# Shorter chains for identity, lengths and mask in the first group, roots in nine operations, and a tie between query scaling and late weights

## The chip, the cores and the metric

The kernel runs on one core of a Trainium2 chip. The metric is device time in microseconds of one execution, from first to last instruction with what lies around them. A core has a matrix engine (TensorE, PE; its weight loads are listed as PEld), a vector engine (VectorE, DVE), an activation engine (ScalarE, ACT), a general engine (GpSimd, POOL), and SyncE (SP), which here issues nearly all DMAs. Each engine works through its own queue in order. TensorE writes to PSUM, which has eight banks[...].

## The reference, cut to what matters

A stack of four graph layers with residual and layer norm, on x of 3327 x 256 and an adjacency matrix of 3327 x 3327. The change touches the first layer, a masked attention with cosine scores, and the inverse square root that all layers use:

```python
def _cos_normalize(x):
    n = jnp.linalg.norm(x, axis=-1, keepdims=True)
    return x / jnp.maximum(n, COS_EPS)
Qn = _cos_normalize(features @ Wq.T)
Kn = _cos_normalize(features @ Wk.T)
raw_att = Kn @ Qn.T
att = jnp.where(adj > 0, raw_att, NEG) * TEMP
att = jax.nn.softmax(att, axis=1)
prop_fea = att @ features
adj_mask = (jnp.sum(adj, axis=1) > 0).astype(features.dtype)[:, None]
prop_fea = adj_mask * prop_fea + (1.0 - adj_mask) * features
# ... then 0.5 * prop_fea + 0.5 * features, and
x = _layernorm(x + _L0_gnn_ref(x, adj, L0_gnn_Wq, L0_gnn_Wk), axis=-1)
```

The later layers (a graph attention, a dot-product attention, three stacked graph attentions) follow with the same mask.

## The kernel before, in words

The 3327 rows are padded to NT = 26 tiles of 128. A block b is a group of four tiles (512 columns; the last has two), so there are NB = 7 blocks. For every layer and block a loop runs over the 26 tiles j. One step (layer, b, j) makes the weights e of tile j against block b, and multiplies them with the value tile V[j] into PSUM accumulators po. In layer 0 `weights0` makes e: a matmul ps of FT[j // 4] (half 0, unscaled) against FT[b] (half 1, normalized), an exponential on ACT whose scale is the inverse length rq of tile j, and a product with the 0/1 mask on DVE. `make` runs three steps ahead of the products (LA = 2, plus one). Blocks 1 to 5 of layer 0 and all of layer 2 use a seven-product scheme: two steps' weights are joined by sums on DVE (`sums`) and used together on the odd step, so on even steps no e is taken from the queue.

Before block 0 can start, the kernel must have: an identity matrix for transposes (a row count, doubled on DVE, four matmuls on TensorE that turn it, and a comparison; eight warm-up matmuls on a tile of ones run ahead of them, L80); FT[0], from `queries0(0)` and `keys0(0)`; the first mask; and the first tiles of x. `queries0` makes the projections pk, sums their squares on ACT, takes inverse lengths (`lengths`, which calls `rsqrt`), scales (L364 on DVE, L366 on ACT), transposes (pkT, L370) and copies to FT[g][:, 1] (L371). `keys0` makes the projection pq (L305), squares it (L312), copies it to FT[g][:, 0] (L313), sums the squares over partitions by matmuls pn (L317), and turns them into rq. Both are generators: each `next` traces the part up to the next `yield`. For g = 0 they are interleaved by hand; for g > 0 parts of them run beside the steps of the block before, and `queries0` takes its inverse lengths on GpSimd, followed by 4 (g = 1) or 7 bare yields until the scaling.

`rsqrt` starts from the integer trick and makes three Newton steps: 11 instructions on DVE, 14 on GpSimd, each waiting for the one before; `lengths` adds a maximum in front.

`take_adj` turns a stage of adjacency (two tiles, 128 x 1024 int32) into a mask of bytes, on DVE for the first eight tiles of block 0 (L408), on ACT (Relu, Sign: L411, L412) otherwise, and adds the stage to a running sum on DVE (L416, L420). `load_adj` loads the next stage; there are three stage buffers.

What sets the order: up to step 3 of the first block the engines PE, ACT, DVE and POOL keep the order in which instructions are written. After that a scheduler orders each engine's instructions, by the written order among those that it takes to be ready by its own model of durations; so an instruction whose inputs it believes to be early can be moved ahead of others on its engine. DMAs queue on SP in order. PSUM: five banks for po, three for everything else (`bank`), given out as they come free.

Of the kernel before, what the change touches and what calls it, by code (L numbers as in the profile page):

```python
# [8 lines left out]
F32 = mybir.dt.float32  # L9
# [4 lines left out]
AF = mybir.ActivationFunctionType  # L14
# [19 lines left out]
def gnn_stack(ctx: ExitStack, tc: tile.TileContext, a: dict, N: int, out: bass.AP):  # L34
# [15 lines left out]
    def bw(b):  # L50
        return min(CH, NP - b * CH)
# [14 lines left out]
    def bank(name):  # L66
        return ps_b.tile([P, CH], F32, tag="pb", name=name)
# [8 lines left out]
    nc.vector.memset(ones, 1.0)  # L76

    turned = bank("turned")
    for _ in range(8):
        nc.tensor.matmul(turned[:, :P], ones, ones, start=True, stop=True)  # L80

    count = const.tile([P, P], F32, name="count")
    nc.vector.memset(count[:, 0:1], 1.0)
    n = 1
    while n < P:
        nc.vector.tensor_scalar(
            count[:, n : 2 * n], count[:, :n], float(n), None, ALU.add
# [43 lines left out]

    def rsqrt(dst, v, n, eng=nc.vector, tag="rs"):

        g = cols.tile([P, n], I32, tag=tag + "_g", name="rs_g")
        eng.tensor_scalar(g, v.bitcast(I32), -0.5, MAGIC, ALU.mult, ALU.add)
        y = g.bitcast(F32)
        vh = cols.tile([P, n], F32, tag=tag + "_v", name="rs_v")
        eng.tensor_scalar(vh, v, -0.5, None, ALU.mult)
        for k in range(3):
            q = cols.tile([P, n], F32, tag=tag + "_q", name="rs_q")  # L140
            eng.tensor_tensor(q, y, y, ALU.mult)
            eng.tensor_tensor(q, q, vh, ALU.mult)
            z = dst if k == 2 else cols.tile([P, n], F32, tag=tag + "_y", name="rs_y")
            if eng is nc.vector:
                eng.scalar_tensor_tensor(z, q, 1.5, y, ALU.add, ALU.mult)
            else:
                eng.tensor_scalar(q, q, 1.5, None, ALU.add)
                eng.tensor_tensor(z, q, y, ALU.mult)
            y = z


    def times(wt, v):
# [114 lines left out]
    def setups():  # L267
        for g in (setup1(), setup2(), setup3a()):
            yield from g
            yield  # L270
# [23 lines left out]
    def lengths(dst, v, n, eng=nc.vector, tag="rs"):  # L294

        eng.tensor_scalar(v, v, COS_EPS * COS_EPS, None, ALU.max)
        rsqrt(dst, v, n, eng, tag)

    def keys0(g):

        wd, n = bw(g), len(tiles_of(g))
        xT = xTs[g]
        pm = bank("pq")
        for h in range(2):
            nc.tensor.matmul(  # L305
                pm[:, :wd], w["qk"][:, h, :H], xT[:, h, :wd], start=(h == 0), stop=(h == 1)
            )
            if g == 1 and h == 0:
                yield
        yield  # L310
        sq = work.tile([P, CH], F32, tag="u", name="qsq", bufs=2)
        nc.scalar.activation(sq[:, :wd], pm[:, :wd], AF.Square)  # L312
        nc.scalar.copy(FT[g][:, 0, :wd], pm[:, :wd])  # L313
        yield
        pn = bank("pn0")
        for k in range(n):
            nc.tensor.matmul(  # L317
                pn[:, k : k + 1], sq[:, k * P : (k + 1) * P], ones[:, :1], start=True, stop=True
            )
        yield  # L320
        v = cols.tile([P, 4], F32, tag="qss", name="qss")
        nc.scalar.copy(v[:, :n], pn[:, :n])
        lengths(rq[:, 4 * g : 4 * g + n], v[:, :n], n)

    def queries0(g):

        wd, n = bw(g), len(tiles_of(g))
        xT = xTs[g]
        ss = cols.tile([P, 4], F32, tag="kss", name="kss")
        kr = work.tile([P, 4, H], F32, tag="kr", name="kr", bufs=1)  # L330
        banks = [bank("pk") for _ in range(2 if g == 0 else 1)]
        for k in range(n):
            pk = banks[k // 2 if g == 0 else 0][:, k * H : (k + 1) * H]
            for h in range(2):
                nc.tensor.matmul(
                    pk,
                    xT[:, h, k * P : (k + 1) * P],
                    w["qk"][:, h, H:],
                    start=(h == 0),
                    stop=(h == 1),  # L340
                )
        if g > 0:
            nc.scalar.copy(kr.rearrange("p k n -> p (k n)")[:, :wd], banks[0][:, :wd])
            yield
        src = [
            banks[k // 2][:, k * H : (k + 1) * H] if g == 0 else kr[:, k, :] for k in range(n)
        ]
        for k in range(n):
            jk = work.tile([P, H], F32, tag="sq0", name="sq", bufs=1)
            nc.scalar.activation(jk, src[k], AF.Square, accum_out=ss[:, k : k + 1])  # L350
        yield
        rk = cols.tile([P, 4], F32, tag="rk", name="rk")
        if g == 0:
            lengths(rk[:, :n], ss[:, :n], n)
        else:
            lengths(rk[:, :n], ss[:, :n], n, nc.gpsimd, "prs")
            for _ in range(4 if g == 1 else 7):
                yield
        yield
        for k in range(n):  # L360
            if g > 0 and k == 2:
                yield
            if g == 0 and k >= 2:
                nc.vector.tensor_scalar(kr[:, k, :], src[k], rk[:, k : k + 1], None, ALU.mult)  # L364
            else:
                nc.scalar.mul(kr[:, k, :], src[k], rk[:, k : k + 1])  # L366
        yield
        pt = bank("pkT")
        for k in range(n):
            nc.tensor.transpose(pt[:, k * P : (k + 1) * P], kr[:, k, :], ident)  # L370
        nc.scalar.copy(FT[g][:, 1, :wd], pt[:, :wd])  # L371
# [7 lines left out]
    def mask(b, j, n=1):  # L379
        wd = bw(b)  # L380
        return masks[b][:, j * wd : (j + n) * wd]
# [21 lines left out]
    def take_adj(b, j):  # L403

        wd = bw(b)
        st = stages.pop((b, j))[:, : 2 * wd]
        if b == 0 and j < 8:
            nc.vector.tensor_scalar(mask(b, j, 2), st, 0, None, ALU.is_gt)  # L408
        else:
            t_ = work.tile([P, 2 * CH], BF16, tag="a", name="pos", bufs=3)  # L410
            nc.scalar.activation(t_[:, : 2 * wd], st, AF.Relu)  # L411
            nc.scalar.activation(mask(b, j, 2), t_[:, : 2 * wd], AF.Sign)  # L412
        if j == 0:
            acc = work.tile([P, CH], I32, tag="u", name="acc", bufs=2)
            adj_sum[b] = acc[:, :wd]
            nc.vector.tensor_tensor(adj_sum[b], st[:, :wd], st[:, wd:], ALU.add)  # L416
        else:
            acc = adj_sum[b]
            for h in range(2):
                nc.vector.tensor_tensor(  # L420
                    acc, acc, st[:, h * wd : (h + 1) * wd], ALU.add
                )
# [30 lines left out]
    def weights0(b, j):  # L453
        wd = bw(b)
        if j % 2 == 0:
            take_adj(b, j)
            load_adj()
        ps = bank("ps")
        nc.tensor.matmul(  # L459
            ps[:, :wd],  # L460
            FT[j // 4][:, 0, (j % 4) * P : (j % 4 + 1) * P],
            FT[b][:, 1, :wd],
            start=True,
            stop=True,
        )
        t_ = work.tile([P, CH], F32, tag="a", name="ex", bufs=3)

        nc.scalar.activation(  # L468
            t_[:, :wd], ps[:, :wd], AF.Exp, scale=rq[:, j : j + 1]
        )  # L470
        return masked(b, j, t_)

    gq = {}

# [730 lines left out]
    load_adj()  # L1205
    masks[0] = new_mask(0)
    k0, q0, q1 = queries0(0), keys0(0), keys0(1)
    for part in (k0, q0, k0, q0, q0, k0, k0, q0, q1):
        next(part, None)
    make(0)  # L1210
    next(q1)
    make(1)
    prep = iter(())
    kprep = iter(())
    setup = setups()
    pre = iter(())

# [10 lines left out]
    for s, (L, b, j) in enumerate(steps):  # L1228
# [29 lines left out]
        if L.key == "0" and b < NB - 1:  # L1258
# [6 lines left out]
            if j >= at + 3:  # L1265
                next(kprep, None)
        es = None if end else made.popleft()
        if end:

            k, h = divmod(2 * j, NT)  # L1270
            for i in (h, h + 1):
                nc.tensor.matmul(  # L1272
                    pos[k],
                    made[i][:, k * P : (k + 1) * P],
                    V[1][i],
                    start=(i == 0),
                    stop=(i == NT - 1),
                )
            if j == 0:
                xm = fetch_last()  # L1280
            if j == NT // 2 - 1:
                ends.append(finish_last(pos[0], xm, 0))
            if ends:
                next(ends[0], None)
        elif not strassen(L, b):
            for k in range(len(pos)):
                nc.tensor.matmul(  # L1287
                    pos[k],
                    es[:, k * P : (k + 1) * P],
                    V[L.i % 2][j],  # L1290
                    start=(j == 0),
                    stop=(j == NT - 1),
                )
        elif j % 2:
            products(pos, b, j // 2, es, V[L.i % 2])
# [115 lines left out]
```

## Time and profile before

| what | value |
|---|---|
| time, median of 3 runs (lowest to highest) | 2379.34 us (2378.32 to 2379.5) |
| the profiled execution's own time | 2376.0 us |
| its span | 2374.2 us |
| mean granted clock of TensorE | 0.998 |
| HBM read, written | 167.53 MB, 28.19 MB |
| first matmul; first L1287 matmul (po) | 1.05 us; 16.38 us |
| POOL memset of 1 column; of 256 columns | 98 ns; 0.31 to 0.34 us |

The time of the profiled execution is some 3 us below the median of the runs, so sums are made against the former. TensorE's busy share is 9 tenths or more in all 40 slices but the last:

```profile
PE   9999999999999999999999999999999999999997
DVE  7889999866666657567567685556656555655665
ACT  4667776765555422222222255555655555655554
POOL 0000001000000000000000000000000000000000
```

Each digit is the busy share of one fortieth of the span (59 us), in tenths. The start shows in the DMA view of the first 60 us: the transfers run at some 370 GB/s from about 3 us to 14 us and with gaps after that. By the semaphores in the trace the projection weights have landed at 4.52 us, the first half of xT's first group at 4.85, its second half at 5.59, the first stage of adjacency at 8.36, the second at 11.13, the third at 12.46.

### The profile page before, as it was taken

How to read it: one execution, taken by the hardware profiler on the slowest of the kernel's cores; microseconds unless marked ns; L12 is line 12 of the kernel's file. 1: busy time of each engine (PE TensorE's matmuls, PEld its weight loads, DVE VectorE, ACT ScalarE, POOL GpSimd, SP SyncE). 2: the span in 40 equal slices, each digit the busy share in tenths (PEclk: the TensorE clock that was granted, in tenths of full speed). 3: DMA queues.
4: the chain of work that ended last, by engine and by line, in shares of the span. 5: the costliest groups of instructions: out<-in, count | busy, mean ns of one | idle time of the engine just before them, and what ended most of it. 6: DMA issues, size and time to landing. Idle time of an engine off the chain costs nothing.

```text
span 2374.2 us, 33168 instructions
## 1 busy us (share of the span) xinstructions
PE 2345.3 (99%) x11965; PEld 1913.6 (81%) x11965; DVE 1608.6 (68%) x4318; ACT 1221.7 (51%) x1959; POOL 42.0 (2%) x168
## 2 busy tenths in 40 slices
PE   9999999999999999999999999999999999999997
PEld 6777877888888777667667798888888888888886
DVE  7889999866666657567567685556656555655665
ACT  4667776765555422222222255555655555655554
POOL 0000001000000000000000000000000000000000
PEclk9999999999999999999999999999999999999999
DMA  8655555422232312212212221210211111132120
GB/s 264 197 180 185 168 196 180 158 84 83 74 83 57 105 56 87 79 53 88 74 49 73 82 85 50 73 52 26 76 47 43 43 59 52 43 98 69 60 66 23
DMA packets 147288, 214.66 MB, mean 90 GB/s; under 512 B 76093, under 2 KB 101172, under 8 KB 142516
## 3 DMA queue, kind: packets, MB, share of 16 engines
q1 hardware_dynamic: 146852, 212.28, 28.9%
q8 instruction: 94, 1.54, 0.3%
q14 instruction: 70, 0.57, 0.1%
q10 hardware_dynamic: 272, 0.26, 0.0%
HBM read 167.53 MB, written 28.19 MB: 82 GB/s over the span
## 4 chain that ended last, share of the span: by engine, by line
PE 89%; DVE 6%; ACT 2%; DMA 2%; issue 1%; POOL 0%; DVEq 0%; ACTq 0%; SPq 0%; POOLq 0%
PE po L1287 49%; PE po L739 17%; PE ps L523 12%; PE ps L459 4%; PE pproj L948 4%; DVE e L448 1%; PE pv L1034 1%; DMA turned<-planes 1%; PE pgq L482 1%; DVE acc L420 1%; PE po L1272 1%; DMA stage<-in_adj_a 1%; DVE ejunk L551 1%; PE pq L305 0%; DVE y L882 0%
## 5 line engine op out<-in xcount | busy, mean ns | idle before, releaser
L1287 PE MATMUL po<-v,e 128*128 128x257 f32 x5616 | 1251.8, 381 | 1.9 <-ACT p L917 1.1
L1287 PEld LDWEIGHTS po<-v,e 128*128 128x128 f32 x5616 | 1062.1, 190 | 169.2 <-issue 9.6
L617 ACT ACTIVATE re<-u,nrh,th 128x512 f32<-128x512 f32 (+1 forms) x728 | 556.4, 780 | 482.7 <-DVE e L628 477.9
L628 DVE SCALAR_TENSOR_TENSOR e<-re,rh,mask 128x512 f32<-128x512 f32 (+1 forms) x702 | 502.3, 719 | 376.7 <-PE po L1287 353.4
L448 DVE SCALAR_TENSOR_TENSOR e<-ex,mask 128x512 f32<-128x512 f32 (+1 forms) x364 | 235.3, 649 | 197.1 <-ACT ex L531 158.2
L523 PE MATMUL ps<-gT,ft 128*128 128x512 f32 (+1 forms) x728 | 307.4, 563 | 0.0
L531 ACT ACTIVATE ex<-ps,off 128x512 f32<-128x512 f32 (+1 forms) x182 | 119.0, 655 | 355.6 <-PE ps L523 329.0
L739 PE MATMUL po<-tsums,ssum 128*128 128x128 f32 (+1 forms) x1794 | 250.9, 275 | 1.7 <-DVE ssum L689 1.4
L739 PEld LDWEIGHTS po<-tsums,ssum 128*128 128x128 f32 x1794 | 224.8, 192 | 3.6 <-DVE ssum L689 3.0
L739 PEld LDWEIGHTS po<-v,e 128*128 128x128 f32 x1196 | 169.4, 191 | 69.2 <-issue 52.9
L523 PEld LDWEIGHTS ps<-gT,ft 128*128 128x128 f32 x728 | 132.1, 190 | 114.5 <-issue 111.7
L739 PE MATMUL po<-v,e 128*128 128x129 f32 x1196 | 182.7, 275 | 1.8 <-DVE e L448 1.8
L468 ACT ACTIVATE ex<-ps,rq 128x512 f32<-128x512 f32 (+1 forms) x182 | 118.0, 653 | 108.2 <-PE ps L459 99.4
L459 PE MATMUL ps<-ft,ft 128*128 128x512 f32 (+1 forms) x312 | 142.7, 562 | 1.1 <-ACT ex L468 1.1
L420 DVE CUSTOM_DVE_ANT_0 acc<-acc,stage 128x1024 uint16<-128x1024 uint16 (+1 forms) x168 | 108.7, 647 | 10.3 <-DMA stage<-in_adj_a 6.4
L739 PE MATMUL po<-v,ssum 128*128 128x128 f32 x598 | 92.3, 275 | 0.0
L739 PE MATMUL po<-tsums,e 128*128 128x128 f32 x598 | 92.2, 275 | 0.0
L412 ACT ACTIVATE mask<-pos 128x1024 uint8<-128x1024 bf16 (+1 forms) x87 | 86.3, 992 | 2.0
L411 ACT ACTIVATE pos<-stage 128x1024 bf16<-128x1024 int32 (+1 forms) x87 | 85.6, 983 | 1.5 <-DVE e L448 1.5
L948 PE MATMUL pproj<-w_l_w,pT 128*128 128x256 f32 x304 | 78.5, 381 | 4.3 <-DVE pT L804 4.3
L739 PEld LDWEIGHTS po<-v,ssum 128*128 128x128 f32 x598 | 79.4, 192 | 0.1
L739 PEld LDWEIGHTS po<-tsums,e 128*128 128x128 f32 x598 | 79.3, 192 | 0.0
(245 smaller groups left out, 1735.9 us busy)
## 6 DMA issues: line engine op xcount, KB each, us to landing
mask<-mask_d SPq DMA_DIRECT2D x30, 1664.0 KB
stage<-in_adj_a SPq DMA_DIRECT2D x78, 512.0 KB
tsums<-t_d SPq DMA_DIRECT2D x152, 256.5 KB
mask_d<-mask SPq DMA_DIRECT2D x6, 1664.0 KB
u<-s_d SPq DMA_DIRECT2D x24, 256.0 KB
xT<-in_xT SPq DMA_DIRECT2D x10, 512.0 KB
mask<-mask_d SPq DMA_DIRECT2D x5, 832.0 KB
t_d<-tsums SPq DMA_DIRECT2D x14, 256.5 KB
```

What stands on the lines that cost most here:

```text
L412: nc.scalar.activation(mask(b, j, 2), t_[:, : 2 * wd], AF.Sign)
L420: nc.vector.tensor_tensor(acc, acc, st[:, h * wd : (h + 1) * wd], ALU.add)
L448: nc.vector.scalar_tensor_tensor(e[:, :wd], t_[:, :wd], 0.0, mask(b, j), ALU.add, ALU.mult)
L459: nc.tensor.matmul(ps[:, :wd], FT[j // 4][:, 0, (j % 4) * P : (j % 4 + 1) * P], FT[b][:, 1, :wd], start=True, stop=True,)
L468: nc.scalar.activation(t_[:, :wd], ps[:, :wd], AF.Exp, scale=rq[:, j : j + 1])
L523: nc.tensor.matmul(ps[:, :wd], FT[j // 4][:, h, (j % 4) * P : (j % 4 + 1) * P], g[:, h, :wd], start=(h == 0), stop=(h == 1),)
L531: nc.scalar.activation(t_[:, :wd], ps[:, :wd], AF.Exp, bias=off, scale=1.0 / D**0.5)
L617: nc.scalar.activation(t_[:, :wd], self.u[b][:, :wd], AF.Relu, bias=self.nrh[:, j : j + 1], scale=self.th[:, j : j + 1],)
L628: nc.vector.scalar_tensor_tensor(e[:, :wd], t_[:, :wd], self.rh[:, j : j + 1], mask(b, j), ALU.add, ALU.mult,)
L739: nc.tensor.matmul(o, x, y, start=(p == 0 and g not in banks[:i]), stop=(p == NT // 2 - 1 and g not in banks[i + 1 :]),)
L948: nc.tensor.matmul(pm[:, :D], pT[:, h, :], w[L.w][:, h, :], start=(h == 0), stop=(h == 1),)
L1287: nc.tensor.matmul(pos[k], es[:, k * P : (k + 1) * P], V[L.i % 2][j], start=(j == 0), stop=(j == NT - 1),)
```

## The change

- Identity: 4 warm-up matmuls in place of 8; the row count starts from eight single-column memsets instead of one, so four doublings remain of seven.
- `rsqrt`: one step of third order and one Newton step in place of three Newton steps: 9 instructions on DVE instead of 11, 12 on GpSimd instead of 14.
- First group: the order of the parts of `queries0(0)` and `keys0(0)`. The copy to FT[0][:, 0] moves behind the matmuls pn and the scaling; the maximum reads pn from PSUM, without the copy on ACT.
- `queries0(g)`, g > 0: before the scaling a new DVE instruction multiplies rk by a comparison (e >= 0, which is always 1) on four columns of the e that was taken last, and the scaling reads its result.
- `take_adj` makes the masks of j = 0 and 2 of block 0 on GpSimd; the running sum becomes a function of its own, `add_adj`, which runs behind the next load, and for j = 0 and 2 behind the product with the mask.
- `weights0` for the very first step makes its exponential and its product in two halves of 256 columns.

```diff
-    for _ in range(8):
+    for _ in range(4):
         nc.tensor.matmul(turned[:, :P], ones, ones, start=True, stop=True)
 
     count = const.tile([P, P], F32, name="count")
-    nc.vector.memset(count[:, 0:1], 1.0)
-    n = 1
+    n = 8
+    for k in range(n):
+        nc.vector.memset(count[:, k : k + 1], k + 1.0)
     while n < P:
...
-        eng.tensor_scalar(vh, v, -0.5, None, ALU.mult)
-        for k in range(3):
-            q = cols.tile([P, n], F32, tag=tag + "_q", name="rs_q")
-            eng.tensor_tensor(q, y, y, ALU.mult)
-            eng.tensor_tensor(q, q, vh, ALU.mult)
-            z = dst if k == 2 else cols.tile([P, n], F32, tag=tag + "_y", name="rs_y")
+        eng.tensor_scalar(vh, v, -0.5 * 0.375**3, None, ALU.mult)
+
+        def step(out, q, c, f):
+
             if eng is nc.vector:
-                eng.scalar_tensor_tensor(z, q, 1.5, y, ALU.add, ALU.mult)
+                eng.scalar_tensor_tensor(out, q, c, f, ALU.add, ALU.mult)
             else:
-                eng.tensor_scalar(q, q, 1.5, None, ALU.add)
-                eng.tensor_tensor(z, q, y, ALU.mult)
-            y = z
+                h = cols.tile([P, n], F32, tag=tag + "_h", name="rs_h")
+                eng.tensor_scalar(h, q, c, None, ALU.add)
+                eng.tensor_tensor(out, h, f, ALU.mult)
+
+        q = cols.tile([P, n], F32, tag=tag + "_q", name="rs_q")
+        eng.tensor_tensor(q, y, y, ALU.mult)
+        eng.tensor_tensor(q, q, v, ALU.mult)
+        p = cols.tile([P, n], F32, tag=tag + "_p", name="rs_p")
+        step(p, q, -10.0 / 3.0, q)
+        z = cols.tile([P, n], F32, tag=tag + "_y", name="rs_y")
+        step(z, p, 5.0, y)
+        q = cols.tile([P, n], F32, tag=tag + "_q", name="rs_q")
+        eng.tensor_tensor(q, z, z, ALU.mult)
+        eng.tensor_tensor(q, q, vh, ALU.mult)
+        step(dst, q, 1.5 * 0.375, z)
...
-        nc.scalar.copy(FT[g][:, 0, :wd], pm[:, :wd])
+        if g > 0:
+            nc.scalar.copy(FT[g][:, 0, :wd], pm[:, :wd])
         yield
         pn = bank("pn0")
...
-        nc.scalar.copy(v[:, :n], pn[:, :n])
-        lengths(rq[:, 4 * g : 4 * g + n], v[:, :n], n)
+        if g == 0:
+            nc.scalar.copy(FT[g][:, 0, :wd], pm[:, :wd])
+            yield
+            nc.vector.tensor_scalar(v[:, :n], pn[:, :n], COS_EPS * COS_EPS, None, ALU.max)
+            rsqrt(rq[:, 4 * g : 4 * g + n], v[:, :n], n)
+        else:
+            nc.scalar.copy(v[:, :n], pn[:, :n])
+            lengths(rq[:, 4 * g : 4 * g + n], v[:, :n], n)
...
+            r2 = cols.tile([P, 4], F32, tag="rk2", name="rk2")
+            nc.vector.scalar_tensor_tensor(
+                r2[:, :n], gate[0][:, :n], 0.0, rk[:, :n], ALU.is_ge, ALU.mult
+            )
+            rk = r2
...
-        st = stages.pop((b, j))[:, : 2 * wd]
+        st = stages[b, j][:, : 2 * wd]
         if b == 0 and j < 8:
-            nc.vector.tensor_scalar(mask(b, j, 2), st, 0, None, ALU.is_gt)
+            eng = nc.gpsimd if j < 4 else nc.vector
+            eng.tensor_scalar(mask(b, j, 2), st, 0, None, ALU.is_gt)
...
+    def add_adj(b, j):
+
+        wd = bw(b)
+        st = stages.pop((b, j))[:, : 2 * wd]
         if j == 0:
...
             take_adj(b, j)
             load_adj()
+        soon = (b, j) in ((0, 0), (0, 2))
+        if j % 2 == 0 and not soon:
+            add_adj(b, j)
...
+        e = work.tile([P, CH], F32, tag="e", name="e", bufs=5)
+
+        n = 2 if (b, j) == (0, 0) else 1
+        for h in range(n):
+            c = slice(h * wd // n, (h + 1) * wd // n)
+            nc.scalar.activation(t_[:, c], ps[:, c], AF.Exp, scale=rq[:, j : j + 1])
+            nc.vector.scalar_tensor_tensor(
+                e[:, c], t_[:, c], 0.0, mask(b, j)[:, c], ALU.add, ALU.mult
+            )
+        if soon:
+            add_adj(b, j)
+        return e
...
-    for part in (k0, q0, k0, q0, q0, k0, k0, q0, q1):
+    for part in (k0, q0, k0, q0, q0, k0, q0, k0, q0, q1):
...
+        if es is not None:
+            gate[0] = es[0] if isinstance(es, tuple) else es
```

## The prediction

> **What bounds the kernel now.** I read the engine shares first, then the chain of waits over the start, then who waits for whom, then every gap of TensorE with the timeline around it. The shares settle the frame:
>
> ```profile
> PE 2345.3 (99%) x11965; PEld 1913.6 (81%) x11965; DVE 1608.6 (68%) x4318; ACT 1221.7 (51%) x1959; POOL 42.0 (2%) x168
> ```
>
> TensorE has work for 2345.3 of 2374.2 us. Nothing in the change takes work from it after the start, so all that can be won or lost is idle time of PE: 28.9 us, of which 1.05 us lie ahead of its first instruction, some 13 us behind its last one (2361.0 to 2374.2), and 14.3 us in gaps between. The chain of the start:
>
> ```profile
> 1.05 3.45 PE turned L80 x16
> 4.50 0.89 PE turned L93 x8
> 5.39 1.79 PE pk L335 x16
> 7.18 1.73 PE pq L305 x4
> ...
> 10.06 1.05 PE pn L317 x8
> 11.11 0.51 PE pkT L370 x4
> ...
> 14.56 0.70 ACT ex L468
> ```
>
> Columns: start us, us, what. The warm-up and the identity (L80, L93) stand ahead of pk; after pq PE idles until 10.06; from there to the first po at 16.38 it is idle only 0.18 us at 15.31 and some 0.1 us ahead of po. From 16.4 on the chain is PE without a break to 60 us and beyond. The other gaps that matter lie at the scaling of later queries. Waits of ACT from 60 to 410 us, then the timeline of ACT and of PE around the last of them:
>
> ```profile
> ACT kr L366 <- POOL rk L148: 22.1, 6, 5.7
> ```
> ```profile
> 398.16 0.40 ACT L366 ACTIVATE kr<-kr,rk 128x128 f32<-128x128 f32 x1 [5.72 <-POOL rk L148]
> ```
> ```profile
> 400.42 1.12 PE L459 MATMUL ps<-ft,ft 128*128 128x512 f32 x2 [1.10 <-ACT ex L468]
> ...
> 403.81 0.49 PE L739 MATMUL po<-v,e 128*128 128x129 f32 x2 [1.81 <-DVE e L448]
> ```
>
> The reader is to see one cause: the scaling L366 stands in ACT's queue ahead of exponentials, though its roots come from GpSimd 5.72 us later. ACT stands still, and PE runs dry: 1.10 + 1.81 + 0.34 (405.42) = 3.25 us. The same at 129.35 (ACT waits 3.48 us) gives gaps of 0.56 and 0.54 us at 132.7 and 138.5. The other four waits cost PE nothing. Sum in reach: 4.35 us.
>
> One more line is a warning, from the timeline of DVE at 1 to 3 us:
>
> ```profile
> 1.24 1.53 DVE L86 TENSOR_SCALAR count<-count 128x2 f32<-128x2 f32 x1
> ```
>
> Its neighbours take 0.16 to 0.24 us; this one was held some 1.3 us while GpSimd worked through its memsets (0.73 to 3.02).
>
> **What the Trainium skill says.** "SBUF — State Buffer", section "Who interferes with whom": DVE and GpSimd share one SBUF port pair under an exclusive lock; a DVE instruction in a two-port mode, or with two SBUF inputs while GpSimd reads SBUF, waits for the whole GpSimd instruction. The 1.53 us line agrees for memsets; no row shows a long GpSimd read. "TensorE: Matmul & The Clock Gate", Part 1: PE starts at half clock and reaches full clock after a busy window of about 3.4 us that does not start with the kernel. The trace agrees: 16 warm-up pieces in 3.45 us (0.216 each), then 8 in 0.89 (0.111). "GPSIMD Engine Reference", section 7: about 1.9 cycles an element for a contiguous read; with its 1.2 GHz this prices the new mask.
>
> **The change part by part.**
>
> *Identity and warm-up.* Eight memsets (one takes 0.06 us) and four doublings replace one memset and seven doublings. The first doubling is now 8 wide and comes near 1.5 us, inside GpSimd's memsets, so I let it be held to 2.77 as before; then two doublings fewer by about 0.21 us: part is ready 0.45 us earlier, L93 starts at 3.85 instead of 4.34 and ends at 4.75 at full clock. pk can't start before its first half of xT has landed, 4.85 by the trace's semaphores: pk at 4.95 instead of 5.23, a gain of 0.28. Four warm-up matmuls fewer leave PE idle from about 2.9 to 3.85. If the clock then stays low until the next window (about 7.2), L93 takes 8 x 0.214 = 1.7 and half of pk is slow: the last pk comes near 8.1 instead of 7.0. Bounds: -0.28 and +0.7 us; I take -0.28, because pk is bound by its data anyway, and keep +0.7 for the range.
>
> *Roots in nine.* The first chain on DVE runs 12 instructions from 8.08 to 10.22, one per 0.197 us; two fewer make -0.39 us. The scaling that follows now ends at 10.88 - 0.28 - 0.39 = 10.2. The other 40 root chains on DVE lie beside PE's work and are worth nothing by themselves (at most 0.4 us at one layer boundary, kept as a bound).
>
> *Order of the lengths.* The copy to FT[0] moves behind the scaling on ACT. In before, pn starts only at 10.06, released by that copy (L313), although its own input was there at 9.53: pn was waiting for pq's bank; the three banks were held by two pk and pq. Now none of the three is free before the scaling ends. So pn starts at 10.2 + 0.06 = 10.26, 0.2 later than before, and pkT behind it. From pn to po PE has 0.91 + 0.47 + 5 x 0.86 = 5.7 us of work; Exp would start near 13.65, half an e is there near 14.5, a bank for the third ps near 14.4, and the PE queue reaches po only at 16.0 to 16.1. The shorter mask, halves and direct read of pn thus stop being the limit: po at 16.1 against 16.38, -0.3 us for the whole start.
>
> *Mask on GpSimd.* It leaves DVE's path (0.69 us a pair, already counted), but its stage lands at 8.36 and the root chain runs 7.8 to 9.55. Price: below, the memset of 256 columns (0.32 us against 0.10 for one) scales to 1.0 us; the skill's 1.9 cycles give an estimate of 1024 x 1.9 / 1.2 GHz = 1.6, with issue 1.7 us; a form twice as slow would be 3.4. Every root instruction is of a kind that the lock holds. Bounds on the path: 0 (no overlap) to 3.4; I take the full 1.7. The second mask (stage lands at 11.13) falls on scaling and a PSUM read, and its cover is PE's 1.5 us of queue ahead of po. Start in all: -0.3 + 1.7 = +1.4 us.
>
> *Halves, sums put back, SP.* One more Exp and product of about 0.38 us each lie under PE's queue. The first sum frees its stage near 15.6 (before: 15.67), the second near 18.95 (18.81); behind the load on SP wait only x tiles for matmuls near 45 us. Nothing. If that cover went, the cost would be the 0.1 us.
>
> *The gate.* r2 on DVE needs e of a step consumed before it, so the scaling can't be hoisted to right behind the squares. GpSimd's chain took 4.9 to 6.9 us and loses two of 15 instructions; e is made some 2.5 to 4 steps of 2.4 us later. Behind r2 on DVE stand the next products; it adds six instructions of 0.16 us. I take 3.7 of the 4.35 us as won; bounds 1.1 (only the wait's place changes, from ACT to DVE) and 4.35.
>
> Sum: +1.4 - 3.7 = **-2.3 us**, against the profiled execution: 2374.2 to 2371.9 of span, 2376.0 to 2373.7 of time. The median of the runs shown is 2379.34, 3.3 above the profiled one; I put the same difference on it: **2377.0 us**.
>
> **The rivals.**
>
> *A, the forecast:* the gate pays, the shared port takes a part back. Its own range: start +0.4 to +2.3, gate -4.35 to -2.5, so 2375.4 to 2379.1.
>
> *B, no collision:* GpSimd's mask slips past the root chain, the whole gate is won and a layer boundary gains 0.5: -0.3 - 4.35 - 0.5 = -5.2, 2374.1 us. For it: the mask could land between two chains. Against: 8.36 lies in the middle of the first.
>
> *C, the wait only moves:* r2 waits for GpSimd on DVE, products and PE stall there, or the new order gives back elsewhere; of the gate 1.1 remains: +1.4 - 1.1 = +0.3, 2379.6 us. For it: at 393.96 one GpSimd instruction of the chain took 1.54 us beside a busy DVE. Here the change would not do what it says.
>
> *D, GpSimd's mask holds the port and sets e:* with a duration d the first root chain loses d, and above 3.8 us the second chain loses it too: a start of 2d - 4.1. With the gate's 3.7 it is slower than before from d = 4.0; at d = 6.5 it is +8.9 - 3.7 = +5.2, 2384.5 us. For it: no row shows such an instruction. Against: it needs 7 cycles an element.
>
> **How the numbers follow.** A 0.52, B 0.13, C 0.25, D 0.10. About 0.2% (4.8 us) is what a measurement of this kernel can tell from no change. Faster by more than that: most of B, 0.11; slower: most of D and a tail of C in which the later order costs a few us, 0.09; the rest, 0.80, within. The range 2374.0 to 2381.5 takes in A, C and the near part of B.
>
> **What would show it.** Right: no wait of ACT for rk over 1 us in 60 to 410 us, and the gaps of PE at 132 and 400 us gone; one root instruction near 8.5 to 9 us of over 1 us; pn released by the scaling, not by the square; first po between 16.5 and 18.5 us. L93 pieces of 0.11 or 0.21 us apart decide on the clock. The forecast is wrong if the first po comes before 15.5, if the GpSimd mask takes over 4 us, if DVE waits for rk instead of ACT, or if new gaps of PE beyond 3 us stand after 410 us, where only roots changed.

## The result, and the profile after

| | before | after |
|---|---|---|
| median, 14 runs each, taken together | 2379.42 us (2376.77 to 2381.58) | 2374.45 us (2372.57 to 2377.88) |
| ratio, 95% interval | | 0.9980 [0.9972, 0.9989] |
| the profiled execution's own time; span | 2376.0; 2374.2 | 2374.08; 2372.3 |
| first po matmul | 16.38 us | 19.27 us |

The change gains 4.97 us; 2.3 were forecast. 2374.45 lies inside the range 2374.0 to 2381.5, near its lower end and next to case B (2374.1). The interval lies below 1, so there is a gain; whether it is more than the 0.2% (4.8 us) that the forecast took for the least that can be told stays open, since the interval reaches to both sides of it.

Two parts are to be seen at once. The shares of the page after, then ACT's waits from 60 to 410 us (line, what it waited for, us in total, times, longest):

```profile
PE 2346.0 (99%) x11957; PEld 1914.3 (81%) x11957; DVE 1598.1 (67%) x4243; ACT 1223.5 (52%) x1959; POOL 43.5 (2%) x158
```
```profile
ACT kr L391 <- DVE rk L380: 8.0, 4, 4.2
```

PE's work is what it was; DVE lost 75 instructions and 10 us. The scaling no longer waits 22.1 us for GpSimd's roots, but 8.0 us for the new product L380, 4.2 us at the longest. PE's gaps at 132, 138, 400 and 403 us are gone: from 110 to 420 us PE idles 0.56 us, where it idled 4.70. Ahead of that there is more idle time than before: 0.58 us at 82.8 us, where there was none, and 2.06 at 97.0, where there were 0.75.

The start went the other way. The timeline of after from 0 to 21 us, in part (start, us, engine, line, operation; in brackets the idle time before it and who ended it):

```profile
3.70 2.08 PE L94 MATMUL turned<-part,count 128*128 128x128 f32 x8 [0.57 <-DVE part L92]
5.57 2.46 PE L354 MATMUL pk<-w_l_wqk,xT 128*128 128x128 f32 x16
...
11.39 1.05 PE L330 MATMUL pn<-ones,qsq 128*128 128x1 f32 x8 [1.65 <-ACT kr L391]
...
13.85 1.91 PE L493 MATMUL ps<-ft 128*128 128x512 f32 x2
15.10 5.56 POOL L434 TENSOR_SCALAR mask<-stage 128x1024 uint8<-128x1024 int32 x2 [12.07 <-issue]
17.95 1.60 DVE L507 SCALAR_TENSOR_TENSOR e<-ex,mask 128x256 f32<-128x256 f32 x2 [3.72 <-POOL mask L434]
19.27 2.00 PE L1331 MATMUL po<-v,e 128*128 128x257 f32 x8 [0.31 <-DVE e L507]
```

Three things stand in it. L94 (L93 in before) runs its eight passes at half clock: 2.08 us, where before's timeline has 1.06. The clock first rises at 6.64 us here, and at 4.01 in the profile of before. pn waits 1.65 us, released by the scaling. And the mask, whose stage had landed at 8.36, starts only at 15.10; the product e waits for it and po for e. Between pn and po the clock was also halved once more. The windows of after (bounds, length, busy time and count of PE, PEld, DVE, ACT, POOL, granted clock, DMA share, GB/s):

```profile
13.00:14.00 1.00, 1.00 (x3) 0.39 (x2) 0.83 (x6) 0.56 (x1) 0.00 (x0) 0.73 1.05 384
14.00:15.00 1.00, 1.00 (x3) 0.48 (x2) 0.19 (x2) 0.00 (x0) 0.00 (x0) 0.50 0.47 162
```

The two ps passes at 13.85 take 1.91 us in that stretch; in the run with the copy first, at full clock, the same two take 1.10. The clock records give the stretch 3.41 us (13.5 to 16.9 here), and the same length to every other one told of below, but for the last one of each run, which starts where PE's work ends. (Up to the first rise of the clock this column shows 1.00 whatever the clock is; there the spacing of the passes tells: 0.21 us for a half, 0.11 for the full clock.)

### The profile page after: what moved, and what is told of

Its sections match the earlier page's. It is cut to its first block, busy times and chain, and to the rows that moved or that the text cites. A ratio compares the mean times of both kernels' runs of the same rounds, so it can differ in the third digit from the quotient of the medians.

```text
span 2372.3 us, 33071 instructions
## 1 busy us (share of the span) xinstructions
PE 2346.0 (99%) x11957; PEld 1914.3 (81%) x11957; DVE 1598.1 (67%) x4243; ACT 1223.5 (52%) x1959; POOL 43.5 (2%) x158
## 4 chain that ended last, share of the span: by engine, by line
PE 89%; DVE 5%; DMA 3%; ACT 2%; issue 1%; POOL 0%; SPq 0%; DVEq 0%; ACTq 0%
PE po L1331 47%; PE po L780 18%; PE ps L564 12%; PE ps L493 4%; PE pproj L989 3%; DMA stage<-in_adj_a 1%; PE pv L1075 1%; DMA turned<-planes 1%; DVE e L507 1%; PE pgq L523 1%; PE po L1316 1%; DVE acc L451 1%; ACT re L658 1%; DVE ejunk L592 0%; DVE v L669 0%
```

## The experiments

**How the profiles are compared.** Every profile has 9906 po matmul passes in the same number, so the start of the n-th can be set against that of before's profile. The table gives this lag in us at the first po and at 102 us (before's time), then its growth over three stretches, and the lag at the last po. It is worked out from the traces.

| kernel | first po | at 102 | 128 to 406 | 406 to 455 | 455 to end | last po |
|---|---|---|---|---|---|---|
| before, again | 1.49 | 2.64 | -0.19 | +1.13 | +0.12 | 3.70 |
| roots alone | 2.40 | 2.67 | +3.40 | +1.18 | -5.83 | 1.42 |
| gate alone | 0.00 | 0.27 | -4.69 | +0.01 | -0.80 | -5.21 |
| roots and gate | 1.51 | 4.80 | -5.16 | +1.41 | -2.90 | -1.85 |
| change without gate | 2.55 | 3.56 | +2.75 | +2.04 | -6.67 | 1.68 |
| change | 2.89 | 5.08 | -5.14 | +1.32 | -3.16 | -1.90 |
| change, again | 2.55 | 9.46 | -5.84 | +1.37 | -3.02 | 1.97 |
| masks on DVE | 2.58 | 5.80 | -5.27 | +1.41 | -3.17 | -1.23 |
| copy first | 2.05 | 2.25 | -4.72 | +1.38 | -2.48 | -3.57 |
| GpSimd early | 1.81 | 6.11 | -5.95 | +1.36 | -3.20 | -1.68 |
| three edits back | 2.14 | 3.11 | -5.79 | +1.39 | -3.03 | -4.32 |
| the same with filler | 0.91 | 1.69 | -5.43 | +1.44 | -4.41 | -6.71 |
| gate and filler | 0.90 | 1.40 | -4.60 | -0.01 | -2.59 | -5.80 |

The first row is the warning: the same kernel in another execution lags by 3.70 us, 1.06 of them grown after 128 us. So one profile says where time goes, and the runs say how much.

### The kernel before once more

No edit.

> The kernel before, unchanged, for a second profile of it. The first profiled execution (2376.0 us) lies below all other times of that kernel. Theory 1 (the size of the gain is hidden by that one good execution): this profile shows a span of 2376 to 2378 us, with the 2 to 3 us more at the start, as a stretch of half clock of PE or a later first po than 16.38. Theory 2 (the span before is right, and the medians differ by what lies outside the profile): a span of 2374 to 2375 us and first po within 0.3 us of 16.38.

Measured 2381.13 us (13 runs), ratio 1.0003 [0.9995, 1.0012]: no change, as it must be. Its profile lags by 1.49 us from the start, because the clock first rises at 7.15 us instead of 4.01. Windows from 3 to 6 us, of before's first profile and then of this one:

```profile
3.00:6.00 3.00, 3.00 (x24) 3.00 (x24) 1.21 (x7) 0.00 (x0) 0.03 (x1) 1.00 1.06 384
```
```profile
3.00:6.00 3.00, 3.00 (x16) 3.00 (x16) 0.91 (x6) 0.00 (x0) 0.02 (x1) 1.00 1.07 384
```

PE is busy throughout in both, and makes 24 passes in the one and 16 in the other. The profile also shows what the idle stretch near 400 us can bring besides:

```profile
405.00:406.00 1.00, 0.21 (x1) 0.21 (x2) 1.00 (x5) 1.00 (x2) 0.00 (x0) 1.00 0.00 0
406.00:407.00 1.00, 1.00 (x7) 0.96 (x7) 1.00 (x4) 1.00 (x2) 0.00 (x0) 0.75 0.00 0
407.00:408.00 1.00, 1.00 (x6) 0.77 (x5) 1.00 (x4) 0.97 (x2) 0.00 (x0) 0.50 0.00 0
```

Right behind the gaps the granted clock falls to 0.50 for 3.41 us, in which the lag grows from 1.98 to 3.18 us. The shown profile of before has the gaps, but not this.

### The gate alone

```diff
+            r2 = cols.tile([P, 4], F32, tag="rk2", name="rk2")
+            nc.vector.scalar_tensor_tensor(
+                r2[:, :n], gate[0][:, :n], 0.0, rk[:, :n], ALU.is_ge, ALU.mult
+            )
+            rk = r2
```

> The kernel before with the gate alone (old roots, old start). Theory 1 (the gate is the gain): ratio 0.9980 to 0.9985, no wait of ACT for rk over 1 us between 60 and 410 us, no gap of PE over 0.5 us at 132 to 138 and 400 to 405 us. Theory 2 (the gate only moves the wait, the gain comes from start or roots): ratio 0.9995 to 1.0005, and DVE or ACT wait for rk as long as before.

Measured 2374.52 us (before, same chip: 2380.36), ratio 0.9970 [0.9959, 0.9980]; the medians differ by 5.84 us. (The ratio is not the quotient of the medians, 0.9975 here.) That is more than either theory allowed, and ACT's longest wait for rk is 1.3 us instead of under 1. ACT's waits of this run:

```profile
ACT kr L372 <- DVE rk L361: 5.1, 5, 1.3
```

The gate alone gains as much as the whole change. Its start is before's to the hundredth (first po 16.38), and all of its gain in the profile lies from 128 to 406 us (-4.69) and after 455 us (-0.80). DVE does not stand waiting for rk: near 130 us GpSimd delivers rk at 130.66, and the product takes it at 133.94.

### Roots and gate, without the edits of the start

The kernel before with the gate and the new `rsqrt`.

> The kernel before with gate and roots in nine, old start: the change without its edits to the first group. Theory 1 (the start edits lose about 2.9 us, as the profile after shows with po at 19.27): faster than the whole change by 2 to 3 us, ratio 0.9965 to 0.9973, first po near 16.0. Theory 2 (the start edits gain, and the profile after met a rare phase of the clock): slower than the whole change by 0.5 to 2 us, ratio 0.9982 to 0.9990.

Measured 2374.65 us, ratio 0.9974 [0.9963, 0.9984]. It is 5.71 us below before, the whole change 4.97 below its own: the edits of the start cost 0.7 us by the medians, which the intervals do not tell from nothing. The first theory's 2 to 3 us and its first po near 16.0 were missed: po came at 17.89, behind a half clock from 11.8 to 15.2 us. Nor is it faster than the gate alone on the same chip (2374.52 us): beside the gate the new roots show no gain in the runs.

### The change without the gate

The six lines of r2 are taken out of after.

> The whole change without the gate (start and roots stay). Theory 1: slower than the kernel before by 1 to 3 us (1.0005 to 1.0012), waits of ACT for rk of 4 us and more are back and the gaps of PE near 400 us too. Theory 2: 0.9980 to 0.9990, nearly the whole gain without the gate.

Measured 2377.99 us, ratio 0.9994 [0.9985, 1.0002]: not slower than before, as the first theory had it, but the gain is not told from nothing. The wait is back at its old size, and behind it stand the same gaps of 1.06 and 1.81 us (406 and 409 us) and a half clock of 3.41 us from 410.6. ACT's waits of this run:

```profile
ACT kr L385 <- POOL rk L149: 23.0, 6, 5.7
```

### The roots alone

> The kernel before with the roots in nine operations alone. Theory 1 (two instructions fewer on the first chain, the rest hidden): 0 to 1 us faster, ratio 0.9995 to 1.0000, ACT still waits for rk 3 to 6 us in all six places. Theory 2 (shorter chains everywhere pay at layer boundaries): 0.9985 to 0.999.

Measured 2378.72 us (before, same chip: 2380.64), ratio 0.9991 [0.9983, 0.9999]: a gain of 1.9 us that just stands clear of nothing, between what the two theories had. The table tells where. It loses 3.40 us from 128 to 406, where the wait of ACT is now 24.4 us, and 1.18 up to 455, and wins 5.83 later: PE's gaps ahead of pproj at 794, 1699, 1873, 2019, 2096 and 2292 us (0.45 to 0.68 us each in before) are under 0.25 us or gone. From 128 us on the sum is -1.25; with the gate (-6.65 of both against -5.48 of the gate) it is -1.17. Two profiles of before differ by 1.06 over the same stretch, so neither sum stands clear of that. In the change itself three of those six gaps are there again, with roots and gate five. Why the gate brings them back was not tried; the scheduler that orders the instructions of both is a candidate, no more.

### The change once more

> The whole change unchanged, for a second profile of it and a ratio beside the others on the same chip. Theory 1: first po again at 18.2 to 19.3 us, the mask on GpSimd again begun 11 to 12 us after its program load, half clock met or not by the phase; ratio 0.9975 to 0.9985, behind the version with three edits back. Theory 2 (the first profile of it met a rare phase): first po near 16, ratio 0.9965 or less.

Measured 2375.76 us (14 runs), ratio 0.9981 [0.9973, 0.9989]: the first result repeats. In its profile PE waits 3.34 us up to 101.8 us for the sum of the adjacency rows (0.75 us in before), and 1.17 at 75. DVE's timeline of this run and of after shows what that sum itself waited for, in one line each:

```profile
99.28 1.42 DVE L451 CUSTOM_DVE_ANT_0 acc<-acc,stage 128x1024 uint16<-128x1024 uint16 x2 [2.47 <-DMA stage<-in_adj_a]
```
```profile
96.59 1.42 DVE L451 CUSTOM_DVE_ANT_0 acc<-acc,stage 128x1024 uint16<-128x1024 uint16 x2 [1.57 <-DMA stage<-in_adj_a]
```

The sum waits for a stage of adjacency to land, as it did in before (1.70 us there, up to 91.50). The loads are late from the start on: the fourth is issued at 19.87 us here and at 20.21 in after, at 15.70 in before. Whether that makes this landing late was not tried; against it, with the copy first the fourth load is issued at 19.37, and PE waits 0.91 us for the sum. The lag at 102 us runs from 0 to 4.80 with the old start and from 3.56 to 9.46 with the new.

### The masks on DVE again

```diff
-            eng = nc.gpsimd if j < 4 else nc.vector
+            eng = nc.vector
             eng.tensor_scalar(mask(b, j, 2), st, 0, None, ALU.is_gt)
```

> The whole change with the masks of the first four tiles back on DVE. Theory 1 (GpSimd's mask, 2.8 us long and not started before 14.8 to 15.1 us, holds the first product and then takes the port from it): the first product starts within 0.2 us of the first half of the exponential, first po at 16.6 to 17.5 us, or near 18.8 if PE is at half clock between 13 and 17 us; 0.4 to 2 us faster than the whole change. Theory 2 (the clock of PE alone sets the first po, the mask is hidden): first po 18.8 to 19.3 us as before, same ratio as the whole change (0.998).

Measured 2374.53 us (before, same chip, here and in the next three: 2381.43), ratio 0.9970 [0.9959, 0.9980]; first po at 18.96. The 16.6 to 17.5 of the first theory was missed, and what was named for a half clock came: from 13.8 to 17.2 us the clock was halved. So GpSimd's mask is not what sets po by itself: where the mask is early, the clock holds po at the same place.

### The copy to FT[0] ahead of pn again

```diff
-        if g > 0:
-            nc.scalar.copy(FT[g][:, 0, :wd], pm[:, :wd])
+        nc.scalar.copy(FT[g][:, 0, :wd], pm[:, :wd])
         yield
...
-            nc.scalar.copy(FT[g][:, 0, :wd], pm[:, :wd])
             yield
```

> The whole change with the copy to FT[0] back ahead of pn. Theory 1 (pn waits for a PSUM bank): pn starts right behind that copy, some 1 us after the square, instead of right behind the scaling; the gap of PE ahead of it falls from 1.65 to about 1.1 to 1.2 us, and PE isn't set back to half clock near 13 us. With GpSimd's mask still there the first po stays at 18.9 to 19.3 us. Theory 2 (pn waits for its own data or for ACT's order): the gap stays at 1.65 us.

Measured 2372.48 us, ratio 0.9966 [0.9954, 0.9978]. The start of pn and of po in the timeline of this run:

```profile
11.33 1.05 PE L329 MATMUL pn<-ones,qsq 128*128 128x1 f32 x8 [1.16 <-ACT ft L325]
...
18.43 2.00 PE L1329 MATMUL po<-v,e 128*128 128x257 f32 x8 [1.17 <-DVE e L505]
```

pn is released by the copy again, and waits 1.16 us instead of 1.65. The clock stayed full after its first rise, as it did with the new order in the change again and in the change without the gate. po came only 0.84 us earlier (18.9 to 19.3 were expected), because now the mask on GpSimd (14.26 to 17.07) held it for 1.17 us. This is the run in which the mask is shown to be the limit, and the one before shows the clock as the limit: two things of nearly the same length lie side by side. The interval overlaps with that of the change, and of the 2.83 us by which this profile leads the change's at 102 us, most lie behind the first po.

### GpSimd's first arithmetic early

A 128 x 4 maximum on GpSimd as its second instruction, four of the 52 memsets behind it, the others behind `make(1)`.

```diff
+    first = const.tile([P, 4], F32, name="first")
+    nc.gpsimd.memset(first, 1.0)
+    nc.gpsimd.tensor_scalar(first, first, 0.0, None, ALU.max)
```

> The whole change, with one 128x4 tensor_scalar on GpSimd ahead of its memsets, and the memsets behind the first four moved behind the first mask. Theory 1 (GpSimd's first arithmetic instruction waits some 12 us for its program to be loaded, whatever its data): the small instruction starts near 12.5 to 13 us instead of 0.9, and the mask follows it at once, 2 us earlier than 15.1. Theory 2 (the mask waits for the port that DVE's roots keep taking, up to 14.8 us): the small instruction starts near 1 us, and the mask near 8.4 us or behind the last root.

Measured 2374.38 us, ratio 0.9970 [0.9960, 0.9980]; first po at 18.19. Timeline of POOL and DVE in this run:

```profile
11.45 0.25 POOL L1238 TENSOR_SCALAR first<-first 128x4 f32<-128x4 f32 x1 [10.38 <-issue]
11.81 2.77 POOL L434 TENSOR_SCALAR mask<-stage 128x1024 uint8<-128x1024 int32 x1
...
12.05 0.82 DVE L137 TENSOR_SCALAR rs_g<-qss 128x4 int32<-128x4 int32 x1
12.78 0.15 DVE L140 TENSOR_SCALAR rs_v<-qss 128x4 f32<-128x4 f32 x1
```

The tiny maximum needed nothing but a memset made at 0.73 us, and still began at 11.45 (12.5 to 13 were expected). In the trace GpSimd's instruction MODIFY_POOL_CONFIG stands at 1.1 us here and at 3.05 in after: from it to the first arithmetic pass 10.3 us here, 12.0 in after, 11.7 in the change again, 11.2 with the copy first. It is this start, and not the stage, that sets the mask: here the mask follows 0.1 us behind the maximum. The Trainium skill names such a cost for a first call ("GPSIMD Engine Reference", section 2.1, some 6 us); the traces here agree in kind and show about twice the time.

The run also shows a collision of the kind that the forecast priced, on the second root chain. One root instruction beside the mask took 0.82 us instead of 0.17, the next eight ran at 0.15 to 0.16 while the mask went on to 14.58: a loss of 0.65 us, not the mask's 2.77. "SBUF — State Buffer", section "Who interferes with whom", has the loser wait for the whole instruction; here the measurement says less.

Moving the memsets tests the warning line of the prediction too. DVE's doubling of the row count in after, then here:

```profile
1.16 2.35 DVE L87 TENSOR_SCALAR count<-count 128x8 f32<-128x8 f32 x4
```
```profile
1.15 0.83 DVE L87 TENSOR_SCALAR count<-count 128x8 f32<-128x8 f32 x4
```

The first of the four took 1.62 us beside GpSimd's row of memsets and 0.17 without it. One such memset takes 0.10, so the hold spans many of them, and not one whole instruction, as the forecast had it when it said that this line agrees with the page. L94 starts at 2.92 us instead of 3.70, and po comes 1.08 us earlier.

### Three edits of the start back

Masks on DVE, the copy first, eight warm-up matmuls; the rest of the change stays.

> The whole change with three of its start edits taken back: masks on DVE, copy ahead of pn, eight warm-up matmuls. Kept: the row count from eight memsets, roots in nine, direct read of pn, halves, sums behind products, gate. Theory 1 (these three cost what the start loses): first po at 14.8 to 16.0 us (0.5 to 1.5 us ahead of the kernel before in the same phase of the clock), ratio 0.9965 to 0.9972, the fastest so far. Theory 2 (start edits don't matter within the noise): ratio 0.9974 to 0.998.

Measured 2371.66 us, ratio 0.9965 [0.9953, 0.9978]. First po at 18.52, so the 14.8 to 16.0 was missed. Windows of this run:

```profile
9.00:12.00 3.00, 1.83 (x11) 1.01 (x10) 2.11 (x12) 1.73 (x6) 0.00 (x0) 1.00 0.98 370
12.00:15.00 3.00, 3.00 (x10) 1.68 (x10) 2.10 (x11) 0.58 (x1) 0.00 (x0) 0.68 1.07 374
15.00:18.00 3.00, 3.00 (x6) 1.25 (x5) 1.39 (x3) 0.97 (x3) 0.00 (x0) 0.75 0.12 42
```

PE idles 1.17 us ahead of pn (busy 1.83 of 3), and the clock is halved behind it, from 13.1 to 16.5 us. With masks, copy and warm-up put back, the idle stretch ahead of pn and the half clock behind it remain.

### Work for PE in that idle stretch

The last kernel, and by itself the gate on the kernel before, with five matmuls of ones that nobody reads, written into a po bank not yet in use:

```diff
         yield
+        if g == 0:
+            spare = ps_o.tile([P, CH], F32, tag="po", name="spare")
+            for _ in range(5):
+                nc.tensor.matmul(spare[:, :P], ones, ones, start=True, stop=True)
         pn = bank("pn0")
```

> The version with three start edits taken back, and five 128x128 matmuls on the tile of ones put between pq and pn, in a bank of po that is free there: work that nobody reads, in PE's idle stretch of 1.17 us. Theory 1 (the idle stretch, by its place in the clock's window, sets PE back to half clock for 3.4 us): no half-clock stretch between 9 and 18 us in the record, gap ahead of pn under 0.3 us, first po at 15 to 16.9 us by when the clock first rises; 0 to 1.5 us faster than without it (ratio 0.9955 to 0.9965). Theory 2 (the clock is drawn at random, whatever PE does): half clock near 13 us is still met, ratio as without (0.9965).

> The kernel before with the gate alone and the same five matmuls between pq and pn, old start otherwise. Theory 1: as fast as or up to 1 us faster than the gate alone (0.996 to 0.997), first po at 16.4 to 17.9 us with no half clock after its first rise. Theory 2: the same as the gate alone or slower, since PE's queue is longer by the five (1.0 us) and pn comes later.

Measured 2369.27 us (2368.55 to 2370.38), ratio 0.9953 [0.9940, 0.9965], and 2369.62 us (2369.39 to 2370.28), ratio 0.9954 [0.9940, 0.9967]; before on the same chip 2380.64. Windows of the first:

```profile
9.00:12.00 3.00, 2.95 (x19) 2.04 (x17) 2.12 (x12) 2.08 (x8) 0.00 (x0) 1.00 1.01 394
12.00:15.00 3.00, 3.00 (x15) 1.78 (x15) 2.10 (x11) 0.67 (x2) 0.00 (x0) 1.00 1.07 372
15.00:18.00 3.00, 3.00 (x10) 1.58 (x9) 2.04 (x5) 1.95 (x4) 0.00 (x0) 1.00 0.20 45
```

PE is busy, the clock stays at 1.00 from its first rise (7.09 us) on, 15 passes run from 12 to 15 us where three edits back had 10, and the first po comes at 17.29 (17.28), later than the 15 to 16.9 expected of it. Both are below before and after: a gain of 11.4 and 11.0 us, of which the gate makes 5.8. By the medians the filler adds 4.9 us to the gain of the gate alone, and 2.4 to that of three edits back; the intervals overlap (0.9954 against 0.9970, 0.9953 against 0.9965), but each of the five runs with the filler is faster than every run of the same kernel without it. The times also spread less: 1.8 and 0.9 us over five runs each, where the gate alone has 5.1 over seven. In those seven the time goes with the mean granted clock: 2371.7 us on average in the two runs at 0.998, 2374.3 in three at 0.997, 2375.2 in two at 0.996. The third decimal is coarse: the half clock at the end of each run enters it too, and the kernel with the filler has 0.997 in two of its five runs.

That the filler works by the clock is likely, but not shown to the end. Neither of the two profiles with it has a half clock at the start, but six of the twelve without it have none either. And the gate's profile, from the fastest of its seven runs, has none anywhere before its end: against it the filler's profile has its first po 0.90 us later, and wins 1.79 us after 455 us, for a reason that was not looked for.

## Why the prediction was right or wrong

*Right: what the gate removes.* "I take 3.7 of the 4.35 us as won" was read from the right rows. The gate alone takes PE's idle time from 110 to 420 us from 4.70 to 0.96 us, which is 3.7; the gap of 0.34 us near 400 stays in every profile with the gate. Case C, in which the wait only moves, is out. That it was just 3.7 us of idle time is luck in part, since the forecast took this share without a sum. Its sign "no wait of ACT for rk over 1 us" failed: 1.3 us are left with the gate alone, and 4.2 in the change, at 79 us. PE's new gap of 0.58 us at 82.8 (0.93 in the second profile) stands close behind that one, and is released by ACT; that the wait makes it was not tried.

*Wrong in size: what this is worth.* The term of the sum that failed is the gate's price in time. It was made of gaps alone, and the gate's profile gained 4.69 us in its place and 0.80 later; the medians say 5.84, and the interval of the ratio 4.8 to 9.8. One cause was seen: PE's clock can be halved for 3.41 us behind the idle stretch. That came in two of the four profiles that have the stretch (before's second one and the change without the gate, where the lag grew by 1.20 and 1.28 us), and in none of the ten with the gate. The profile that the forecast was made against had none of it. The other part was measured, but stays open: the lag shrinks by 4.69 where idle time shrinks by 3.7, and most of the difference lies between 129 and 141 us (1.83 of lag for two gaps of 1.10). The bound of 4.35, the sum of the gaps, was too low for both.

*Wrong in size: the roots.* "The other 40 root chains on DVE lie beside PE's work and are worth nothing by themselves" fell. By themselves they are worth 1.9 us by the medians, and the gaps at the layer boundaries are where the profile gains; the bound of 0.4 for one layer boundary was for one of several. Beside the gate the runs show nothing of it (2374.65 against 2374.52 us). For the first chain, -0.39 us was near: its instructions are still 0.2 us apart, and it takes 1.78 us from its first to the scaling, where it took 2.18. But in the old order this moves nothing ahead of pn, which waits 1.16 us for the copy either way; of PE's idle time only the 0.18 us ahead of the third ps go.

*The start: near in size by luck, wrong in mechanism.* +1.4 us was forecast. By the first po the three profiles with the whole start lag by 2.66 us on average and the five with the old one by 1.08, so +1.6; the runs say +0.7 and do not tell it from nothing. Part of the +1.6 is the moment of the clock's first rise, which the forecast had at one place: among the fourteen profiles it comes at 4.01 to 9.67 us, and for the very same kernel at 4.01 and 7.15. Its steps, one by one:

- Identity: "L93 ... ends at 4.75 at full clock" was wrong; the bound "if the clock then stays low" came. The passes took 0.21 us or more each, and pk started at 5.57, not 4.95. But the eight warm-up matmuls do not keep this off: L93 has the same half clock in the second profile of before and in roots alone. The first rise comes at 4.01 to 7.15 us in the eight profiles with eight of them and at 6.13 to 9.67 in the six with four, so fewer may put it off, and more than that is not shown. At the same half clock the shorter identity even gains: pk starts at 5.57 instead of 6.33.
- Order of the lengths: "none of the three is free before the scaling ends" was right. pn is released by the scaling, 0.05 us after ACT's two instructions of it (10.71 and 0.63), as said. Priced as 0.2 us of shift, it adds 0.49 us to PE's idle stretch (1.65 against 1.16). What the forecast left out is the clock behind that stretch. It was halved in three of the five profiles with the order of the change (after, masks on DVE, GpSimd early), but also in three of the seven with the old order and no filler (roots alone, roots and gate, three edits back), so this is not the new order's price alone.
- Mask on GpSimd: "its stage lands at 8.36 and the root chain runs 7.8 to 9.55", so they collide for 1.7 us. There was no collision, as in case B, but not because it slipped between two chains: GpSimd's first arithmetic starts 10 to 12 us behind MODIFY_POOL_CONFIG. The duration was 2.76 to 2.89 us, not the 1.7 of the estimate, though inside the bounds of 0 to 3.4. Then it held e. And the second mask stood beside e's product: of two equal halves one took 1.27 us, the other 0.41.
- Sums put back: "the first sum frees its stage near 15.6 (before: 15.67)" was wrong. The sum stands behind the late product, and the load that it holds back is issued at 20.21 us. What this costs is open; the wait at 97 us is the place to look.
- "The PE queue reaches po only at 16.0 to 16.1" supposed full clock from 3.85 us on. No profile with the edits of the start had it before 6.13, so this was not tested; the two profiles with full clock from 4.01 have the old start, and po at 16.38.

*The rivals.* B's sum (-5.2) met the measured -4.97 for a wrong reason: it won nothing at the start, and more than its 4.35 at the gate. That the measured time lies within the range is owed to the gate and in spite of the start. D's condition (a mask of over 4 us) did not come. (PE's gaps in the profile of before sum to 14.7 us, not 14.3; nothing rests on it.) Of what would show it, the first po "between 16.5 and 18.5 us" came at 19.27, "one root instruction ... of over 1 us" did not come, and the gaps and the release of pn did.

The parts do not add: by the medians -5.8 for the gate, -1.9 for the roots and -2.4 for the change without the gate, against -5.0 for all. The profiles lay this to the wait near 400 us, which the roots alone lengthen and the gate removes, to the pproj gaps that come back with the gate, and to the half clock.

## What to carry to other kernels

Price an idle stretch of TensorE by the gap and by the clock behind it, and look at more than one profile of the kernel before, since the one shown may have met no half clock. Where a short wait of TensorE can't be removed, a few matmuls that no one reads can be worth more than shortening the chain that it waits for. GpSimd's first arithmetic had a price here that no steady row shows; move work to it at the very start only where 10 to 12 us of delay are harmless. Before a delay at the start is put down to an edit, look where the clock first rose in both profiles.

## What the runs showed of the hardware

- TensorE's clock changes on a grid of 3.41 us: in each profile every change lies a whole number of such steps behind the first rise (2 and 3 at the start, 27 and 28 at 97 to 102 us, 117 to 119 at 406 to 414 us). Where the grid lies differs by execution, and with it the first rise: 4.01 and 7.15 us in two profiles of before.
- Half clock came for one step of 3.41 us behind idle stretches far shorter than that: 1.65 us ahead of pn in after, 1.17 in three edits back, 0.92 and 1.81 at 402 to 406 us. In all six profiles that have one at the start, it begins 6.83 us, twice 3.41, after the clock's first rise. The Trainium skill ("TensorE: Matmul & The Clock Gate", Part 1) tells of a window of 3413 ns that runs free of the kernel, which fits both. What must be idle stays open: 1.16 us brought half clock in roots alone and none in before, and PE was busy 0.47 of the step ahead of the half clock at 406.5 us in before's second profile, 0.46 of a step (400.0 to 403.4 us) in its first, behind which the clock stayed full.
- A stretch cost 1.7 us where PE was the limit: at 97 us in roots and gate the lag grew by 3.29, of which 1.63 are the gap (2.37 against 0.74). At 406 us, where PE also had slack, the lag grew by 1.20 (1.28 in the change without the gate).
- GpSimd's comparison of 128 x 1024 int32 into bytes takes 2.76 to 2.89 us; DVE takes 0.69 for the same (683 to 693 ns in after).
- A DVE instruction of 0.17 us was held for 1.62 us beside a row of GpSimd memsets of 0.10 us each; it took 0.17 again when the memsets were moved away.
